# A list scheduler that weaves two layers together: two PSUM banks for the front, ranks of its evictions and of the carried columns' copies

## The chip, the core and the metric

The kernel runs on one core of a Trainium2 chip. The core has five engines with a queue of instructions each: PE (matmul, with its weight loads shown apart as PEld), DVE (vector), ACT (scalar functions), POOL (a second elementwise engine) and SP, which here issues nearly all DMAs. An engine takes its instructions in the order of its queue, and an instruction that waits holds up all that stand behind it. Matmuls write PSUM, which has eight banks of 128 x 512 float32; ACT and DVE read them there, POOL works on SBUF alone. The metric is the device time of one execution in microseconds.

## The reference, cut to what matters

Eight images of 56 x 56 x 192 go through two layers. Layer 0 is an attention whose queries and keys come from depthwise convolutions. Layer 1 is a selective scan in four directions. Everything is float32.

```python
def _L0_conv_ref(x, ...):                     # x is group-normalised before
    q  = _sep_conv(x, dw_q, ..., pw_q, 1)     # depthwise 3x3, batch norm, 1x1
    kv = _sep_conv(x, dw_kv, ..., pw_kv, 2)   # the same with stride 2
    k, v = jnp.split(kv, 2, axis=-1)
    scores = jnp.einsum('bihd,bjhd->bhij', q, k) * SCALE      # 3136 queries, 784 keys, 3 heads
    o = jnp.einsum('bhij,bjhd->bhid', jax.nn.softmax(scores, axis=-1), v)
    return jnp.einsum('bhwc,cd->bhwd', o, out_w) + out_b

def _ss2d(x, ...):                            # x is group-normalised before
    xa, z = jnp.split(jnp.einsum('bhwc,oc->bhwo', x, in_proj_w), 2, axis=-1)
    xc = jax.nn.silu(conv3x3_depthwise(xa) + conv_b)          # 384 channels
    xs = four directions of xc                                # rows, columns, and both reversed
    dts, Bs, Cs = jnp.split(jnp.einsum('bkdl,kcd->bkcl', xs, x_proj_weight), [R, R + N], axis=2)
    delta = jax.nn.softplus(dt_projs(dts) + bias)
    def step(h, inp):                                         # 3136 steps, 16 states per channel
        u_l, d_l, B_l, C_l = inp
        h = jnp.exp(d_l[..., None] * A) * h + d_l[..., None] * B_l[:, :, None, :] * u_l[..., None]
        return (h, jnp.sum(h * C_l[:, :, None, :], axis=-1))
    ...
    y = layernorm(sum of the four directions + xs * Ds) * jax.nn.silu(z)
    return jnp.einsum('bhwd,cd->bhwc', y, out_proj_w)

x = x + _L0_conv_ref(_gn(x), ...)
x = x + _L1_conv_ref(_gn(x), ...)
```

The four directions are put back in the order of the image before they are added.

## The kernel before

**Who sets the order.** The program has no fixed loop nest around its engines. While it is being built, a list scheduler (class `Sched`) runs some dozens of Python generators, called stages. A stage yields a request: an engine, an estimated duration, the cells that it reads and the cells that it writes. It may also ask for a buffer of a ring. The scheduler keeps a planned time for each engine, works out when each request could start, takes the one with the smallest start less rank, and lets its stage emit the instructions. A rank is thus a head start in microseconds: a request of rank 0.36 is taken before one of rank 0.16 as long as it starts no more than 0.2 later. What comes out is a fixed order for each engine; the chip then runs these orders with its own durations.

**The scan** (the stages in the list at line 1375) is a pipeline over `todo`: 8 images x 4 directions x 7 chunks of 448 positions x 16 states. For each of these 3584 steps:

- `inputs_made`: POOL multiplies the step sizes by a broadcast row of B into a state tile h (L1177, 128 x 1344). There are seven h tiles.
- `decays`: ACT makes three exponentials into da (L1191). These lie in PSUM banks.
- `scans`: DVE runs three scans (L1208) over da and h.
- `carries`: DVE copies the last column of h (L1230), from which the next chunk's scan of the same state starts, 16 steps on.
- `turned`, `scaled`, `back`: PE transposes h in four parts into a bank ht (L1255), ACT scales it by the C values (L1271), PE transposes it back and adds it up in three banks y of its own (L1289).
- `by_pool`: for four of the 16 states (three in the last image) POOL does the multiplication by C itself, from the second of a group on in place, into h (L1307), and adds up (L1311). It waits for the carry copy of that state, since the copy reads what L1307 may overwrite. `summed` adds the result into y on PE (L1326).
- `evicted`: DVE adds y to the image's sum (L1341, L1343).

`row_loads` fetches the B and C rows (tiles bb, five of them, and cb) over SP. An h tile is free when the copy and the turning, or the copy and POOL's product, are done.

**The front** is all that comes before the scan of an image: `front` (group norm, the first convolution L641 and L649, the projections L658 to L672, attention L784 and L793, the input projection L899, the second convolution L917) and `x_proj` (L994 to L1011). The front of image 0 and three chunks of its `x_proj` run alone with eight banks. After that, the front of image b + 1 runs beside the scan of image b, and `finish` (layer norm, gate, output projection, L1042 to L1094) beside both.

**Pacing.** `pace` says how much PE time the front should have used by the present place in the scan and how far it is behind. The scheduler skips a request of the front while the front is 12 or more ahead, and gives it a rank of 0.04 per microsecond behind, from 0 up to 0.45. The group of `finish` has a limit of its own, 0 in general.

**PSUM while both run.** Three banks are y. The other five are shared by three claims, each with a limit: da two, ht two, and one for the front and `finish` together. A request for a bank is answered when the claim is under its limit and one of the five is free.

**Fillers.** Where the planner sees PE idle, `warm` puts in small matmuls (L1421) that add zeros to y. One of them shows as two records in the profile.

The ranks of the scan's stages and the shared banks, as they stand before the change:

```python
            rda = share("da", 2)
            rht = share("ht", 2)
            banks[0] = share("bank1", 1)
            at["chunk"] = 0
            for g, rank in ((prepared, 0.3), (skips, 0.0), (row_loads, 0.25), (inputs_made, 0.0), (decays, 0.37),
                            (scans, 0.16), (carries, 0.36), (turned, 0.37), (scaled, 0.38), (by_pool, 0.39),
                            (back, 0.4), (summed, 0.0), (evicted, 0.71)):
```

Of the kernel before, what the change touches and what calls it, by code (L numbers as in the profile page):

```python
# [54 lines left out]
PE, ACT, DVE, POOL, SP = range(5)  # L55
# [3 lines left out]
URGENT = 0.45  # L59
AHEAD = 12.0  # L60
FIRM = 0.04


FILL = 64
# [103 lines left out]
class Sched:  # L168
# [54 lines left out]
    def run(self, until=None):  # L223
        while True:
            moved = True
            while moved:
                moved = False
                for s in list(self.stages):
                    while not s.done and not isinstance(s.req, tuple):
                        if isinstance(s.req, Ring):  # L230
                            if not s.req.ready():
                                break
                            self.resume(s, s.req.take())
                        else:
                            if not s.req():
                                break
                            self.resume(s)
                        moved = True
                    if s.done:
                        self.stages.remove(s)  # L240
                        moved = True
            if (until is not None and until()) or not self.stages:
                return
            best = None
            for s in self.stages:
                if not isinstance(s.req, tuple):
                    continue
                rank = s.rank
                if s.group in self.limit:
                    behind = self.limit[s.group]()  # L250
                    if behind <= -AHEAD:
                        continue
                    rank = max(rank, min(URGENT, FIRM * behind))
                e, _, reads, writes = s.req[:4]
                t = s.start
                for c in reads:
                    if c.w is None:
                        break
                    if c.w > t:
                        t = c.w  # L260
                else:
                    for c in writes:
                        if c.r > t:
                            t = c.r
                    t = max(t + HOP, self.at[e])
                    if best is None or t - rank < best[0]:
                        best = (t - rank, t, s)
            assert best is not None, "nothing can go on"
            _, t, s = best
            if s.req[0] == PE and self.filler is not None:  # L270
                self.keep_busy(t)
            self.give(s, t)
# [3 lines left out]
def kernel(  # L276
# [78 lines left out]
    for nm, src in (("q", bn_q), ("kv", bn_kv)):  # L355
        p = load(f"bn{nm}", [CP, 4, NB], src.rearrange("v (b p) -> p v b", p=CP))
        s = const.tile([CP, NB], F32, name=f"bns{nm}")
# [75 lines left out]
    banks = [None]  # L433
# [914 lines left out]
    with tc.manual_schedule():  # L1348
        order = [(lay, c) for lay in range(2) for c in range(NCH)]

        with tc.tile_pool(name="p8", bufs=8, space=PSUM) as p8:
            banks[0] = Ring(lambda: p8.tile([128, 512], F32, name="bank0"), 8)
            sc.spawn(front(0), 0.0, "front")
            sc.run()
            main = sc.spent.pop("front")
            sc.spawn(x_proj(0, order[:LEAD]), 0.0, "front")
            sc.run()
            each = sc.spent.pop("front") / LEAD

        with ExitStack() as es:  # L1360
            py = es.enter_context(tc.tile_pool(name="py", bufs=1, space=PSUM))
            pb = [es.enter_context(tc.tile_pool(name=f"pb{i}", bufs=1, space=PSUM)) for i in range(5)]
            ybanks = py.tile([128, NJ, 512], F32, name="y")
            nc.vector.memset(ybanks, 0.0)
            ry = Ring(lambda: ybanks, 1)
            shared = [Tile(1) for _ in pb]

            def share(name, most):
                return Share(shared, [lambda p=p: p.tile([128, 512], F32, name=name, tag="bank") for p in pb], most)

            rda = share("da", 2)
            rht = share("ht", 2)
            banks[0] = share("bank1", 1)
            at["chunk"] = 0
            for g, rank in ((prepared, 0.3), (skips, 0.0), (row_loads, 0.25), (inputs_made, 0.0), (decays, 0.37),
                            (scans, 0.16), (carries, 0.36), (turned, 0.37), (scaled, 0.38), (by_pool, 0.39),
                            (back, 0.4), (summed, 0.0), (evicted, 0.71)):
                sc.spawn(g(), rank, "scan")

            per = NDIR * NCH * NST  # L1380

            def ended(b):
                first = b * NDIR * NCH + (NDIR - 1) * NCH
                yield lambda: at["chunk"] >= first
                yield from finish(b, lambda c: lambda: at["chunk"] >= first + NCH - c, yread[b])

            def arounds():
                for b in range(nb):
                    yread[b] = {}
                    sc.spawn(ended(b), 0.0, "finish")  # L1390
                    if b > 0:
                        yield lambda: at["chunk"] >= b * NDIR * NCH
                    else:
                        yield from sc.join([sc.spawn(x_proj(0, order[LEAD:]), 0.0, "front")])
                    if b + 1 < nb:
                        yield from sc.join([sc.spawn(front(b + 1), 0.0, "front")])
                        yield from sc.join([sc.spawn(x_proj(b + 1, order), 0.0, "front")])

            def pace():

                b, slot = divmod(at["scan"], per)
                whole = main + len(order) * each
                lead = each * (len(order) - LEAD)
                before = b * whole + (lead if b else 0.0)
                here = whole + (0.0 if b else lead)
                late, share = (NDIR - 1) * NCH * NST, 0.87
                part = share * slot / late if slot < late else share + (1.0 - share) * (slot - late) / (per - 2 * NST - late)
                want = before + here * part
                return want - sc.spent.get("front", 0.0)

            def ending():
                done = sum(len(r) for r in yread.values())
                b, c = divmod(at["chunk"], NDIR * NCH)
                come = b * NCH + max(c - (NDIR - 1) * NCH, 0)
                return 1e9 if done < come - 1 or done < b * NCH else 0.0

            def warm():

                while True:
                    yield PE, T_FILL, [], []  # L1420
                    nc.tensor.matmul(ybanks[:, 0, T:T + FILL], zeros, zeros[:, :FILL], start=False, stop=False)  # L1421

            def may():
                y = ys.get(at["y"])
                return y is not None and y["left"][0] > 0 and y["on"]

            at["y"] = -1
            filler = Stage(warm(), 0.0, 0.0, None)
            sc.resume(filler)
            sc.filler = filler, may  # L1430
            sc.limit["front"] = pace
            sc.limit["finish"] = ending
            sc.spawn(arounds(), 0.0)
            sc.run()
# [58 lines left out]
```

## Time and profile before

| | |
|---|---|
| runs | 17156.64, 17158.03, 17169.37 us; median 17158.03 |
| the profiled execution | 17147.92 us, span 17146.2 us |
| granted PE clock, mean of that execution | 0.982 |
| h products on POOL, L1177 | x3584, 3054 ns each |
| scans on DVE, L1208 with a carry | x9216, 1136 ns each |
| decays on ACT, L1191 | x10752, 638 ns each |
| scaling on ACT, L1271 | x10864, 579 ns each |
| carry copies on DVE, L1230 | x3584, 158 ns each |
| fillers on PE, L1421 | x12432, 1600.3 us busy |
| HBM | read 1803.75 MB, written 550.97 MB |

How to read the profile: "busy" is the time in which an engine works on an instruction; the idle time before an instruction is put down to the one that released it ("<-"). Neighbours on ACT and DVE overlap a little, so the distance from start to start is shorter than the duration given. The same source line stands five lines further down in the changed kernel (two in the scheduler's first part). A wait put down to "issue" is one for which the profile shows no releaser.

### The profile page before, as it was taken

The numbers are of one execution on the slowest core, as the hardware profiler recorded it, in microseconds if no ns is written. First come the engines' busy times: TensorE is split into PE (matmuls) and PEld (weight loads), VectorE is DVE, ScalarE is ACT, GpSimd is POOL, SyncE is SP. The second block draws the span as 40 slices with busy tenths as digits, with TensorE's granted clock in tenths as the row PEclk, the third lists the DMA queues.
The fourth block names the chain that finished last, engine by engine and source line by source line (L and its number), as shares of the span: only waits on it lengthen the run. The fifth ranks groups of instructions, "written<-read, shape, count | busy, mean of one in ns | idle before, by whom it ended". The sixth has DMA issues, their size and how long they took to land. (4 is left out here: it accounts for less than half of the span.)

```text
span 17146.2 us, 283077 instructions
## 1 busy us (share of the span) xinstructions
PE 15622.8 (91%) x101664; PEld 10978.3 (64%) x101664; DVE 13834.8 (81%) x17783; ACT 14266.4 (83%) x25158; POOL 15542.8 (91%) x5200
## 2 busy tenths in 40 slices
PE   7699999999999999999899999999989999999998
PEld 3366666666666666666666666666666666667776
DVE  2378878888788878888788887888878888789998
ACT  3479888788888888888887888878888788888888
POOL 0389999899998999999898999989989899999998
PEclk9799999999999999999999999999999999999999
DMA  2653455436553365533745337453464534643332
GB/s 73 202 170 105 138 172 170 126 97 169 172 160 109 97 179 164 164 103 95 197 155 156 101 104 203 147 152 99 124 193 142 146 99 137 191 146 104 97 98 79
DMA packets 1508346, 2373.36 MB, mean 138 GB/s; under 512 B 197104, under 2 KB 1498912, under 8 KB 1503872
## 3 DMA queue, kind: packets, MB, share of 16 engines
q1 hardware_dynamic: 1506944, 2355.25, 47.3%
q8 instruction: 808, 13.24, 0.3%
q14 instruction: 594, 4.87, 0.1%
HBM read 1803.75 MB, written 550.97 MB: 137 GB/s over the span
## 5 line engine op out<-in xcount | busy, mean ns | idle before, releaser
L1208 DVE TENSOR_TENSOR_SCAN h<-da,newc,h 128x448 f32<-128x448 f32 x9216 | 10105.2, 1136 | 1535.2 <-ACT da L1191 1080.0
L1177 POOL TENSOR_TENSOR h<-du_s,bb 128x1344 f32<-128x1344 f32 x3584 | 10819.8, 3054 | 296.9 <-PE ht L1255 234.7
L1191 ACT ACTIVATE da<-dl_s,acoef 128x448 f32<-128x448 f32 x10752 | 6625.5, 638 | 766.6 <-DVE h L1208 454.0
L1271 ACT ACTIVATE g<-ht,ct_s 112x384 f32<-112x384 f32 x10864 | 5946.5, 579 | 1125.6 <-PE ht L1255 935.8
L1289 PE MATMUL y<-ident,g 112*128 112x112 f32 x32592 | 4889.8, 269 | 670.7 <-ACT g L1271 434.2
L1255 PE MATMUL ht<-ident,h 128*112 128x128 f32 x32592 | 5212.6, 277 | 232.0 <-DVE h L1208 169.5
L1289 PEld LDWEIGHTS y<-ident,g 112*128 112x128 f32 x32592 | 3524.6, 142 | 2752.1 <-ACT g L1271 1764.6
L1255 PEld LDWEIGHTS ht<-ident,h 128*112 128x112 f32 x32592 | 3699.3, 135 | 1185.9 <-issue 498.3
L1208 DVE TENSOR_TENSOR_SCAN h<-da,h 128x448 f32<-128x448 f32 x1536 | 1602.9, 1078 | 361.9 <-ACT da L1191 276.7
L1307 POOL TENSOR_TENSOR yp<-h,cb 128x1344 f32<-128x1344 f32 x448 | 1367.4, 3052 | 278.2 <-DVE h L1208 124.1
L1421 PEld LDWEIGHTS y<-zeros 128*128 128x128 f32 x12432 | 1553.3, 193 | 78.9 <-issue 78.9
L1421 PE MATMUL y<-zeros 128*128 128x64 f32 x12432 | 1600.3, 269 | 0.0
L1307 POOL TENSOR_TENSOR h<-h,cb 128x1344 f32<-128x1344 f32 x420 | 1282.1, 3053 | 271.3 <-issue 175.4
L1311 POOL TENSOR_TENSOR yp<-yp,h 128x1344 f32<-128x1344 f32 x420 | 1278.7, 3045 | 31.7
L784 PE MATMUL bank<-qT,kT 128*112 128x448 f32 x2352 | 1118.0, 568 | 115.6 <-ACT pT L734 48.7
L978 POOL TENSOR_TENSOR v<-v,xs 128x1344 f32<-128x1344 f32 x224 | 680.2, 3049 | 596.8 <-DMA dl<-v 584.0
L1326 PE MATMUL y<-yp,ident 128*128 128x448 f32 x2688 | 1205.0, 548 | 16.2 <-POOL yp L1311 15.9
L793 PE MATMUL bank<-pT,vt 112*128 112x448 f32 x2352 | 1038.7, 545 | 46.6 <-ACT pT L734 35.0
L734 ACT ACTIVATE pT<-bank,nsh 112x448 f32<-112x448 f32 x1176 | 744.5, 635 | 135.5 <-PE bank L784 118.9
L1011 PE MATMUL bank<-xd,dtw 128*128 128x448 f32 x1344 | 640.2, 561 | 25.1 <-DVE h L1208 12.7
L1230 DVE TENSOR_REDUCE newc<-h 128x3 f32<-128x3 f32 x3584 | 564.9, 158 | 107.8
L784 PEld LDWEIGHTS bank<-qT,kT 128*112 128x112 f32 x2352 | 346.6, 178 | 357.8 <-ACT pT L734 152.2
(147 smaller groups left out, 9664.2 us busy)
## 6 DMA issues: line engine op xcount, KB each, us to landing
bb<-rows SPq DMA_DIRECT2D x3584, 224.0 KB, 3.4
cb<-rows SPq DMA_DIRECT2D x868, 224.0 KB, 3.6
dl<-v SPq DMA_DIRECT2D x224, 672.0 KB, 4.9
du<-v SPq DMA_DIRECT2D x224, 672.0 KB, 6.2
du_s<-du SPq DMA_DIRECT2D x224, 672.0 KB, 4.7
dl_s<-dl SPq DMA_DIRECT2D x224, 672.0 KB, 4.7
stack<-xpd SPq DMA_DIRECT2D x504, 232.0 KB, 5.6
xt<-x1d SPq DMA_DIRECT2D x224, 336.0 KB, 5.0
```

Of the source, the lines that this page charges most:

```text
L784: nc.tensor.matmul(ps.ap[:TP, :T], kts[h][:, kb * TP:(kb + 1) * TP], qh.ap, start=True, stop=True)
L793: nc.tensor.matmul(po.ap[:, :T], vt[:, kb, g:g + 2, :].rearrange("p g d -> p (g d)"), pts[kb].ap, start=(kb == 0), stop=(kb == NKB - 1))
L1177: nc.gpsimd.tensor_tensor(h.ap, du.ap, bb.ap.unsqueeze(1).to_broadcast([128, NJ, T]), ALU.mult)
L1191: nc.scalar.activation(da.ap[:, :T], dl.ap[:, j], AF.Exp, scale=acoef[:, k * NJ + j, n:n + 1])
L1208: nc.vector.tensor_tensor_scan(h.ap[:, j, rev], da.ap[:, 0:T][:, rev], h.ap[:, j, rev], news[i - 1].ap[:, j, n:n + 1] if ci else 0.0, ALU. ...
L1255: nc.tensor.transpose(ht.ap[:TP, j * 128:(j + 1) * 128], h.ap[:, j, s * TP:(s + 1) * TP], ident)
L1271: nc.scalar.activation(g.ap, ht.ap[:TP, :DIN], AF.Copy, scale=ct.ap[:, s, n:n + 1])
L1289: nc.tensor.matmul(y["t"].ap[:, j, s * TP:(s + 1) * TP], g.ap[:, j * 128:(j + 1) * 128], ident[:TP, :TP], is_transpose=True, start=(n == 0 ...
L1307: nc.gpsimd.tensor_tensor(to.ap, h.ap, cbr.ap.unsqueeze(1).to_broadcast([128, NJ, T]), ALU.mult)
L1311: nc.gpsimd.tensor_tensor(yp.ap, yp.ap, h.ap, ALU.add)
L1326: nc.tensor.matmul(y["t"].ap[:, j, :T], ident, yp.ap[:, j], start=False, stop=(y["left"][j] == 0))
L1421: nc.tensor.matmul(ybanks[:, 0, T:T + FILL], zeros, zeros[:, :FILL], start=False, stop=False)
```

## The change

Three edits, all in what the scheduler is told. The front and `finish` may hold two of the five shared banks at once. The limit of a paced group, which applied to each of its requests, now applies only to requests for PE and to those whose estimated duration is over 1.0; the others (evictions of a bank, DMA issues, small vector work) are never held back for being ahead, and their rank is at least 0.2. And the copies of carried columns go from rank 0.36 to 0.25; the scans keep 0.16.

```diff
+EVICT = 0.2
+BRIEF = 1.0
...
                 if s.group in self.limit:
                     behind = self.limit[s.group]()
-                    if behind <= -AHEAD:
-                        continue
-                    rank = max(rank, min(URGENT, FIRM * behind))
+                    if s.req[0] == PE or s.req[1] > BRIEF:
+                        if behind <= -AHEAD:
+                            continue
+                        rank = max(rank, min(URGENT, FIRM * behind))
+                    else:
+                        rank = max(rank, EVICT, min(URGENT, FIRM * behind))
...
-            banks[0] = share("bank1", 1)
+            banks[0] = share("bank1", 2)
...
-                            (scans, 0.16), (carries, 0.36), (turned, 0.37), (scaled, 0.38), (by_pool, 0.39),
+                            (scans, 0.16), (carries, 0.25), (turned, 0.37), (scaled, 0.38), (by_pool, 0.39),
```

The constants here are `AHEAD` 12.0, `FIRM` 0.04 and `URGENT` 0.45.

## The prediction

> **What bounds the kernel now.** I read five views in this order: the page's busy table, the busy time by long stretch, the same by stretches of 100 us over one image, the waits of the engine found there, and the timeline of one such place.
>
> ```profile
> PE 15622.8 (91%) x101664; PEld 10978.3 (64%) x101664; DVE 13834.8 (81%) x17783; ACT 14266.4 (83%) x25158; POOL 15542.8 (91%) x5200
> ```
>
> ```profile
> 7200.00:9200.00 2000.00, 1844.94 (x11861) 1282.30 (x11860) 1651.05 (x2099) 1706.90 (x3006) 1887.37 (x630) 0.98 0.49 141
> 15200.00:16700.00 1500.00, 1361.96 (x10085) 1082.27 (x10084) 1341.38 (x1657) 1338.12 (x2449) 1494.27 (x497) 1.00 0.36 107
> ```
>
> The first line is the page's, the two others are long stretches. In these the pairs are PE, PE's weight load, DVE, ACT and POOL. POOL is the bound: with no front beside it (the last line) it is busy 1494 of 1500 us, with the front 1887 of 2000. PE's 91% flatters: the groups show 12432 filler records of 1600.3 us busy (two to an instruction), work that is put only into gaps, so useful PE work is 82%.
>
> POOL's instructions (5152 products of about 3.05 us) are untouched by the change. What can be won is its idle time: 17146.2 - 15542.8 = 1603 us, of which about 685 lie before the first h product (at 688 us, some set-up on POOL included) and 814 in 1200 to 15200. Where do the 814 lie?
>
> ```profile
> 7100.00:7200.00 100.00, 84.68 (x654) 71.59 (x653) 83.03 (x122) 70.87 (x131) 89.33 (x32) 0.96 0.64 183
> 7200.00:7300.00 100.00, 98.93 (x818) 61.03 (x818) 84.61 (x123) 69.22 (x129) 70.48 (x27) 0.99 0.59 158
> 7300.00:7400.00 100.00, 89.64 (x628) 64.37 (x626) 83.92 (x107) 78.11 (x149) 89.02 (x31) 0.95 0.37 105
> 7600.00:7700.00 100.00, 94.06 (x548) 62.70 (x547) 83.05 (x105) 89.77 (x166) 99.77 (x34) 1.00 0.36 108
> 8300.00:8400.00 100.00, 88.05 (x646) 53.62 (x638) 62.64 (x75) 77.58 (x124) 76.95 (x26) 0.90 0.75 194
> 8400.00:8500.00 100.00, 85.80 (x703) 61.17 (x702) 69.48 (x84) 92.57 (x158) 87.48 (x29) 1.00 0.70 202
> ```
>
> They lie in lumps. From 7100 to 7400 POOL loses 10.7 + 29.5 + 11.0 = 51 us, from 8300 to 8500 another 36; attention between them (7600) loses next to nothing. By line, 7200 to 7310 holds the front's first convolution (L641, L649; PE 98.9% busy), 8300 to 8450 its second (L917). Tagging all stretches of 100 us from 1000 to 15600 by these lines: the first convolution's lose 300.7 us over seven images (405 with their neighbours), the second's 220.3, attention's 156 (2.9 per 100 us), the rest 169.
>
> ```profile
> POOL h L1177 <- PE ht L1255: 16.4, 6, 7.5
> POOL h L1307 <- issue: 10.1, 3, 7.0
> POOL yp L1307 <- DVE h L1208: 9.3, 2, 6.8
> POOL h L1307 <- DVE newc L1230: 7.4, 2, 5.9
> ```
>
> ```profile
> 7225.53 0.64 ACT L1191 ACTIVATE da<-dl_s,acoef 128x448 f32<-128x448 f32 x1 [1.87 <-DVE hkv L595]
> 7227.82 0.72 ACT L614 ACTIVATE hq<-bank,bntq,bnsq 96x448 f32<-96x448 f32 x1 [0.60 <-PE bank L649]
> ```
>
> The first four are POOL's waits in 7100 to 7400 (total, times, longest): no state buffer is free because PE turns states late, or a scan or carry copy is late. The last two are ACT there: a decay waits 1.87 us for the bank that an eviction of the front gives back, then an eviction waits for its matmul.
>
> **What the Trainium skill says.** "Perfetto Trace Analysis", Optimizing Tensor Performance, Matmuls, says that independent groups should rotate through PSUM banks so that evacuation lies beside the next matmuls; the bracketed waits above agree that one bank does not give that. Its Optimization Strategy says to look at regimes apart, and the table by stretch is why. "Trainium Architecture — The Big Picture", Inside one NeuronCore, says that each engine has its own stream and they meet at semaphores; so an order fixed beforehand stalls wherever the chip is later than the plan. In the trace a scan costs 1.08 us from start to start (3.24 for three) against the planner's 1.065, a decay 0.60 against 0.56, a scaling 0.52 against 0.47.
>
> **The change part by part.** The program after has the same instructions on ACT, DVE, POOL and SP; only PE's fillers fall, 6216 to 5785. All else is order, so I compared the two programs' orders, counting place in h products (one each 4.4 us in a front image: 651 POOL instructions x 3.05 / 448). The first image's lone front, 700 us, is untouched.
>
> *Second bank and prompt evictions.* Before, the chunk h 48 to 64 of an image holds 53.9 us of front PE work (each instruction at its mean in the trace) and no filler: the front starts late (inputs turned at h 22 to 29, convolution at 42 to 65), is behind its pace, and takes the rank 0.45 that beats everything of the scan but adding up a chunk. After, inputs are turned at h 5 to 17, the convolution spans 29 to 59, and the densest chunk of that stage has 32.8 us, then 25.9 and 25.1. Attention has 25 us per chunk in both, at 2.9 us of POOL lost per 100 us. Between 25 us costing 2.9 and 53.9 costing 29.5 a line gives about 10 at 32.8; the stage would cost 10 + 3 + 3 = 16 instead of 51, a gain of 35 per image. The 7100 stretch also has the image's boundary, and the two bounds are 0 (the loss only moves) and 51; I take 27. 7 x 27 = 190 us. The second convolution keeps its density (31.6 to 32.9): 0, bounds +-10 per image, +-70 in all. x_proj ends at h 417 instead of spilling to the next image: no engine waited much there, 0.
>
> *What the banks cost.* Five banks now serve 2 + 2 + 2 claims. In building, the front takes its bank with one already held in 2437 of 3399 cases, and ht has to start from none held in 1181 of 10864 (4 before). That can hurt: see the first rival. I take 0 for what the new order has absorbed, with up to +350 kept.
>
> *Evictions past the pace.* What is not on PE and costs under 1.0 also goes on when the front is ahead. On SP these are DMAs (0.32 us each to issue); the lead of the bb loads over the h products is the same in both orders (lead of one: 353 and 350 times), so bb's 23.3 us of waits should stay: 0, up to +40. On ACT and DVE rank 0.2 still stands under decays (0.37) and scalings (0.38) but over scans (0.16): a scan late by one 0.6 us copy is hidden by DVE's 17% idle.
>
> *Carries.* Before, every copy L1230 follows its own third scan; after, 1686 of 3131 follow the next step's first scan. It removes a stall that the planner sees (0.13 us after the scan) and the trace hardly does: 107.8 us idle over 3584 copies, on an engine that is not the bound: 0 to -50. Behind the copy wait POOL's in-place products L1307. If 54% of the 49 + 81 waits of 1200 to 15200 that are named newc or issue grow by one scan, 0.54 x 130 x 1.08 = 76 us; the new order may put the product later, then 0. I take +20.
>
> *Last image.* No front, but 1267 fillers instead of 1098: 169 x 0.257 = 43 us of PE. PE has 138 us idle in the 1500 there and POOL binds: 0, at worst +43. *The end:* finish may hold two banks, -2 us at most, taken as 0.
>
> Sum: -190 + 20 - 20 (fewer waits of attention's evictions, 0 to -60 from its 156) = -190. The profiled execution took 17147.9, span 17146.2; that gives 16958. The median of the runs is 10 us above it, so I say 16965. The fillers speak for the same size: a front image has 100 fewer (719 to 619), 100 x 0.257 = 26 us less room on PE per image, though they are a plan's gaps and not the chip's.
>
> **The rivals.** *The turning loop loses its second bank (slower).* While the front holds two banks and the decays two, ht has one, and PE's turn, ACT's scaling and the hand-overs run one after another: 0.49 + 0.58 + about 0.2 = 1.27 us per tile. A front chunk allows 23 x 3.05 / 48 = 1.46. If one decay of 0.60 stands in the loop every other time, it is 1.57, 0.11 too much; the share of decays taken in that state is 3655 of 10752, 34%, so of 7 x 28 x 48 = 9408 tiles 3200 pay 0.11: 350 us, less the 190 won, and 17320. It decides from 1.46 us per tile. For it: POOL already waits 217 us for PE's turns in 1200 to 15200. Against: that order was made with the banks counted.
>
> *The loss only moves (no change).* The front's PE work per image is the same, and the chip's lateness against the plan may make as many holes spread as in lumps: 17150. Against: attention shows that 25 us per chunk goes nearly free.
>
> *Both convolutions heal (larger gain).* With two banks ACT no longer meets the matmul at the bank, and POOL loses attention's 3% everywhere: 350 + 70 = 420 us, 16740. Against: the second convolution also waits for its stack loads.
>
> *The banks do nothing* is excluded by the 2437 second takes.
>
> **How the numbers follow.** Forecast 0.53, from 16850 to 17080 or a little above; larger gain 0.15; no change 0.07; slower 0.25. The runs of a kernel differ by some 0.1%, and what can be told from no change is 0.2%, 34 us. Faster 0.68, same 0.07, slower 0.25. With 16760 to 17240 I leave out the larger gain's end (0.06) and the worse half of the slower case (0.13).
>
> **What would show it.** Right: POOL's busy stays at 15540; in the stretches of the first convolution it loses under 15 us per 100 instead of 30; the second still loses about 12 to 23; PE's fillers fall to 11570 records. Wrong: waits of L1177 for ht at L1260 well above 235 us, or ACT's scalings waiting longer than 936 us for PE, mean the loop; waits of L1312 for the copies above 170 us mean the carries; holes of POOL inside attention mean that the loss moved.

## The result and the profile after

The changed kernel took 17014.25 us, the median of four runs (17000.83 to 17024.88), against 17159.81 before: a ratio of 0.9914 with a 95% interval of 0.9897 to 0.9931. That is 0.86% less, 146 us. The profiled execution has a span of 16999.1 us, 147.1 shorter. Three lines of its page and of its stretches answer to the first ones of before; the pairs are again PE, PE's weight load, DVE, ACT and POOL.

```profile
PE 15535.8 (91%) x100802; PEld 10839.1 (64%) x100802; DVE 13629.1 (80%) x17783; ACT 14233.1 (84%) x25158; POOL 15540.0 (91%) x5200
```

```profile
7200.00:9200.00 2000.00, 1845.02 (x11786) 1280.26 (x11786) 1646.89 (x2128) 1717.61 (x3026) 1902.93 (x637) 0.98 0.48 144
15200.00:16700.00 1500.00, 1361.56 (x10511) 1124.82 (x10509) 1325.33 (x1670) 1331.40 (x2494) 1495.11 (x498) 1.00 0.33 101
```

POOL is as busy as before, 15540 us. Nearly the whole difference is its idle time: 17146.2 - 15542.8 = 1603 before, 16999.1 - 15540.0 = 1459 after, 144 us less. So the question is which holes in POOL went. One image of after, in stretches of 100 us:

```profile
7000.00:7100.00 100.00, 90.63 (x707) 69.10 (x708) 82.44 (x122) 80.79 (x147) 91.83 (x35) 0.98 0.74 220
7100.00:7200.00 100.00, 96.78 (x750) 63.18 (x744) 79.86 (x115) 75.69 (x143) 76.08 (x26) 0.98 0.46 135
7200.00:7300.00 100.00, 84.93 (x621) 59.03 (x620) 92.79 (x113) 74.92 (x142) 97.74 (x33) 0.95 0.41 122
8100.00:8200.00 100.00, 94.86 (x613) 54.37 (x611) 84.12 (x109) 74.84 (x133) 84.06 (x29) 0.99 0.89 237
```

The first three hold the first convolution: POOL loses 8 + 24 + 2 = 34 us where it lost 51. The lump is smaller, but it is there; the last line begins the second convolution. Tagged as in the prediction, over all stretches from 1000 to 15600:

| POOL idle, us | before | after |
|---|---|---|
| first convolution (with the neighbouring stretches) | 300.7 (405) | 267.1 (348) |
| second convolution | 220.3 | 223.8 |
| attention | 156.2 | 103.1 |
| the rest | 169.0 | 122.2 |
| sum | 846 | 716 |

The tags move a little: the second convolution has 23 stretches after and 18 before, the rest 52 and 58, so part of the rest's fall is a change of tags.

What is left of the lump looks different. POOL's waits in 7000 to 7300 of after (total, times, longest), and then lines of the timeline of its longest hole (start, duration, idle before):

```profile
POOL h L1312 <- issue: 24.8, 4, 14.3
POOL h L1312 <- DVE newc L1235: 5.0, 3, 3.8
POOL h L1182 <- PE ht L1260: 4.0, 3, 2.4
```

```profile
7103.53 0.22 DVE L613 COPY vt<-bank 112x64 f32<-112x64 f32 x1 [1.36 <-PE bank L669]
7108.04 3.22 DVE L1213 TENSOR_TENSOR_SCAN h<-da,newc,h 128x448 f32<-128x448 f32 x3
7108.15 0.64 ACT L1196 ACTIVATE da<-dl_s,acoef 128x448 f32<-128x448 f32 x1 [2.47 <-DVE hkv L600]
7111.68 1.15 DVE L1213 TENSOR_TENSOR_SCAN h<-da,newc,h 128x448 f32<-128x448 f32 x1 [0.43 <-ACT da L1196]
7112.75 0.37 DVE L600 TENSOR_SCALAR hkv<-bank,bnskv,bntkv 96x112 f32<-96x112 f32 x1
7113.04 0.14 DVE L1235 TENSOR_REDUCE newc<-h 128x3 f32<-128x3 f32 x1
7113.32 3.06 POOL L1312 TENSOR_TENSOR h<-h,cb 128x1344 f32<-128x1344 f32 x1 [14.26 <-issue]
```

The wait named "issue" ends as the carry copy of 7113.04 ends (0.14 us later), so it is a wait for a copy. That holds beyond this hole: of the 66 waits of in-place products named issue in 1200 to 15000, 64 end within 0.3 us after a copy. Before, POOL stood for turns and for copies alike; after, most of what it waits here (30 of 37 us) is the in-place product L1312 behind a late copy.

The copy is late because of what DVE does in these 14.3 us. Besides seven scans it works off eight pieces of the front, some 3.3 us, and waits 1.36 us for the matmul of one of them. The copy itself stands behind the next step's first scan and one more piece: it starts 1.8 us after its own third scan has ended at 7111.26. A decay did wait 2.47 us until DVE had emptied a bank of the front, but DVE runs the three scans from 7108.04 without a break, and its only wait for a decay here is 0.43 us.

### The profile page after: what moved, and what is told of

Its sections match the earlier page's. It is cut to its first block, busy times and chain, and to the rows that moved or that the text cites. A ratio compares the mean times of both kernels' runs of the same rounds, so it can differ in the third digit from the quotient of the medians.

```text
span 16999.1 us, 281592 instructions
## 1 busy us (share of the span) xinstructions
PE 15535.8 (91%) x100802; PEld 10839.1 (64%) x100802; DVE 13629.1 (80%) x17783; ACT 14233.1 (84%) x25158; POOL 15540.0 (91%) x5200
## 5 line engine op out<-in xcount | busy, mean ns | idle before, releaser
L1260 PE MATMUL ht<-ident,h 128*112 128x128 f32 x32592 | 5281.3, 279 | 329.5 <-DVE h L1213 124.3
L1312 POOL TENSOR_TENSOR h<-h,cb 128x1344 f32<-128x1344 f32 x420 | 1284.0, 3057 | 451.0 <-issue 293.8
L1426 PEld LDWEIGHTS y<-zeros 128*128 128x128 f32 x11570 | 1462.0, 196 | 75.2 <-issue 75.2
L1426 PE MATMUL y<-zeros 128*128 128x64 f32 x11570 | 1500.4, 272 | 0.0
L1312 POOL TENSOR_TENSOR yp<-h,cb 128x1344 f32<-128x1344 f32 x448 | 1368.7, 3055 | 102.0 <-DVE h L1213 44.6
L1316 POOL TENSOR_TENSOR yp<-yp,h 128x1344 f32<-128x1344 f32 x420 | 1278.4, 3044 | 32.8
L789 PE MATMUL bank<-qT,kT 128*112 128x448 f32 x2352 | 1077.8, 550 | 57.7 <-DVE h L1213 42.6
L1331 PEld LDWEIGHTS y<-yp,ident 128*128 128x128 f32 x2688 | 438.1, 191 | 177.8 <-issue 160.3
L1235 DVE TENSOR_REDUCE newc<-h 128x3 f32<-128x3 f32 x3584 | 509.3, 142 | 34.3
```

Source lines behind the costliest of these rows:

```text
L789: nc.tensor.matmul(ps.ap[:TP, :T], kts[h][:, kb * TP:(kb + 1) * TP], qh.ap, start=True, stop=True)
L1260: nc.tensor.transpose(ht.ap[:TP, j * 128:(j + 1) * 128], h.ap[:, j, s * TP:(s + 1) * TP], ident)
L1312: nc.gpsimd.tensor_tensor(to.ap, h.ap, cbr.ap.unsqueeze(1).to_broadcast([128, NJ, T]), ALU.mult)
L1316: nc.gpsimd.tensor_tensor(yp.ap, yp.ap, h.ap, ALU.add)
L1331: nc.tensor.matmul(y["t"].ap[:, j, :T], ident, yp.ap[:, j], start=False, stop=(y["left"][j] == 0))
```

## The experiments

Each starts from the changed kernel and puts edits back, or changes one number. All ratios are against the kernel before.

**The three edits alone.** Each of the first three runs keeps one edit of the change and puts the other two back; the fourth puts back the copies' rank alone, by the line shown. Theory A is the prediction's.

> Only the second bank for the front and finish; evictions paced as before, copies at rank 0.36. Theory A (the lumps: the front starts earlier and its first convolution is spread, bank and evictions together do it): about half of the gain, -60 to -120 us against before, and POOL's idle in the stretches of the first convolution falls. Rival B (the carries' lower rank is what gains, since the planner no longer sees a stall of DVE after each third scan): within 40 us of before. Rival C (the turning loop's lost bank costs): slower than before by 50 us or more, and POOL's waits for ht rise above 235 us.

> Only the evictions' own rank and their release from the pace; one bank, copies at rank 0.36. Theory A: -60 to -120 us against before, as the front's start moves from h 22 to h 12 of an image and its densest chunk stays at 53.9 us of PE work. Rival B: within 40 us of before. If the densest chunk sets the loss of the first convolution's stretches, that loss stays near 300 us here and falls in the run with the banks alone.

> Only the copies' rank 0.36 to 0.25. Theory A: slower than before by 50 to 100 us, since POOL's in-place products wait for copies that come one scan later: their waits named newc and issue rise from 313 us in 1200 to 15200 to about 400. Rival B: faster than before by 80 us or more.

```diff
-                            (scans, 0.16), (carries, 0.25), (turned, 0.37), (scaled, 0.38), (by_pool, 0.39),
+                            (scans, 0.16), (carries, 0.36), (turned, 0.37), (scaled, 0.38), (by_pool, 0.39),
```

> The changed kernel with the copies' rank put back to 0.36: both other edits stay. Theory A: faster than the changed kernel by 60 to 100 us (near 16930), with the waits of the in-place products for copies back at about 310 us from 412. Rival B: slower than the changed kernel by 80 us or more (17100 or above).

| kernel | median us | ratio and interval |
|---|---|---|
| second bank alone | 17122.4 | 0.9980 (0.9972 to 0.9987) |
| eviction rank alone | 17119.0 | 0.9976 (0.9968 to 0.9984) |
| copies' rank alone | 17139.4 | 0.9988 (0.9979 to 0.9996) |
| bank and eviction rank, copies back at 0.36 | 16944.5 | 0.9875 (0.9861 to 0.9888) |
| all three (the change) | 17014.3 | 0.9914 (0.9897 to 0.9931) |

Each alone gives 20 to 40 us, less than A expected of the first two and the other sign than it expected of the third. The first two lie in B's range of 40 us, but B also asked for 80 us or more from the third and for 17100 or more with the copies back, and neither came. Nor did C: POOL's waits for turns were 224 us with the banks alone. In the run of the third the waits of POOL's products by C (L1312, those into yp among them) for copies did rise, from 311 to 413 us in 1200 to 15000, but those for a free h tile fell from 217 to 157 and those of the products into yp for scans from 117 to 71. Together, bank and eviction rank give 214 us, nearly three times their sum. And the copies' lower rank, a small gain alone, costs about 70 us on top of the two. The kernel with the copies back beats both kernels of this case. POOL's waits in 1200 to 15000 show the exchange, first before, then in the changed kernel, then with the copies back:

```profile
POOL h L1177 <- PE ht L1255: 217.4, 82, 9.2
POOL h L1307 <- issue: 164.2, 58, 10.0
POOL h L1307 <- DVE newc L1230: 71.7, 32, 8.6
```

```profile
POOL h L1312 <- issue: 266.4, 66, 14.7
POOL h L1312 <- DVE newc L1235: 115.0, 44, 7.8
POOL h L1182 <- PE ht L1260: 91.1, 56, 5.5
```

```profile
POOL h L1312 <- issue: 203.0, 69, 10.0
POOL h L1312 <- DVE newc L1235: 44.6, 40, 2.8
POOL h L1182 <- PE ht L1260: 167.8, 68, 5.5
```

With late copies POOL waits 134 us more at the in-place product and 77 less for a free h tile; 57 us of the 70 are in these three lines.

**Density is worth little.** How long is PE busy with the front while POOL makes 14 h products in a row, at the densest place of the first convolution? In the traces, for the last five of the seven images with a front beside them: 60 us before, 46 to 47 in the change, 45 to 46 with two banks alone, 46 to 50 with the eviction rank alone. Each half spreads the burst about as much as the change does. With the banks alone the first convolution still loses 272 us (372 with the neighbours), which is 29 of the 34 us that the change saves there; with the eviction rank alone it loses 285. So flattening the burst brings some 30 us, and the gain of the pair lies elsewhere:

| POOL idle, us | before | two banks alone | eviction rank alone | both, copies at 0.36 |
|---|---|---|---|---|
| first convolution | 300.7 | 272.2 | 285.3 | 246.5 |
| second convolution | 220.3 | 285.3 | 243.0 | 228.0 |
| attention | 156.2 | 130.1 | 152.4 | 83.7 |
| the rest | 169.0 | 125.6 | 156.0 | 95.9 |
| sum | 846 | 813 | 837 | 654 |

With the banks alone three rows gain and the second convolution loses 65 us. The trace shows where: POOL waits for rows of B, most of it in one hole of 11 to 13 us in the second convolution of five images. The first line is the sum in 1200 to 15000, the others are one of these holes:

```profile
POOL h L1182 <- DMA bb<-rows: 73.6, 11, 12.7
```

```profile
10476.51 2.46 SPq L489 DMA_DIRECT2D xcw<-xw  x2
10488.41 2.06 SPq L489 DMA_DIRECT2D stack<-xpd  x3
10500.05 3.05 POOL L1182 TENSOR_TENSOR h<-du_s,bb 128x1344 f32<-128x1344 f32 x1 [11.80 <-DMA bb<-rows]
```

SP issues nothing from 10478.97 to 10488.41: it waits to issue a stack load of the front until PE's L922 has used the old stack, and the loads of B stand behind it. With the rank beside the banks POOL's waits for B are 2.0 us. So this stall accounts for about 70 of the 159 us of idle time that the rank takes from POOL here; why the order with the rank avoids it was not traced.

**Which queue the rank works on.** Two banks, copies at 0.36, and the rank for one engine's brief requests at a time:

```diff
-                    if s.req[0] == PE or s.req[1] > BRIEF:
+                    if s.req[0] != DVE or s.req[1] > BRIEF:
```

> Two banks, copies at 0.36, and the rank of at least 0.2 only for the front's brief requests on DVE. The two banks alone gave 17122, with the rank on all three queues 16945. Theory D (the rank works through DVE's evictions: 0.2 puts them before the scans' 0.16, so a bank comes back to the turning sooner): most of the 178 us, 17000 or less. Rival S (it works through SP, whose requests fall under the same rank): within 40 us of the two banks alone, 17080 to 17160.

> The same with the rank only for the front's brief requests on ACT. Theory D: 17080 to 17160, since 0.2 still stands under decays (0.37) and scalings (0.38) there. Rival A (ACT's evictions free the banks of the convolutions and of the scores): 17030 or less.

> The same with the rank only for the DMA issues of the front. Theory D: 17080 to 17160, with POOL's waits for the bb rows still near 74 us as with the two banks alone. Rival S: 17030 or less, and those waits fall to 15 us or less as in the run with the copies back.

DVE gave 0.9958 (0.9945 to 0.9972), ACT 0.9972 (0.9961 to 0.9982), SP 0.9973 (0.9965 to 0.9981), against 0.9980 without the rank. DVE has the largest share, 0.22%, but not most of the gain as D expected, and the intervals of ACT and SP overlap that of no rank; the three add up to 0.37% of the 1.05% that the rank brings on all three queues. POOL's wait for the B rows (bb) stayed at 75 us on SP alone, so rival S falls too, and ACT did not reach what rival A asked. With DVE alone these waits were 28 us, with ACT alone 14.

The other half of that edit does nothing. A program in which brief requests are freed from the pace but get no rank of their own is, on all five engines, instruction for instruction the one with the banks alone: the front is never 12 ahead.

**The copies, state by state.**

```diff
             h = states[i, n][0]
+            sc.now.rank = 0.36 if n in by[i] else 0.25
             yield DVE, 0.08, h.c[1:1 + NJ], [news[i].c[n]]
```

> The changed kernel, but the copies of the states that POOL multiplies by C keep rank 0.36; the others have 0.25. Theory W (the copies' lower rank costs because POOL's in-place product waits for a copy that comes one scan later): at or under the 16945 of the run with all copies back, and POOL's waits named newc and issue before the in-place products fall from 412 us to about 300. Rival P (the copies' rank matters through the whole plan, by whatever order comes out): stays within 40 us of the changed kernel's 17014 or above it.

16948.6 us, 0.9882 (0.9868 to 0.9895): the 70 us are back, though in an image with a front 12 of 16 copies keep the lower rank. So the rank of the other four decides the time. That it does so through the products' waits for copies is shown only in part: they fell from 412 to 351 us, where W put about 300.

**Who owns the banks.** The decays get two of the five for themselves (the added numbers are the first bank of a claim and the end of its range):

```diff
-            rda = share("da", 2)
-            rht = share("ht", 2)
-            banks[0] = share("bank1", 2)
+            rda = share("da", 2, 0, 2)
+            rht = share("ht", 2, 2)
+            banks[0] = share("bank1", 2, 2)
```

> Base is the changed kernel with the copies back at 0.36 (16945). Here the decays keep two of the five banks for themselves, and the front and the turning share the other three, two each at most. Theory F (what the second bank brought is that decays no longer wait for the front's evictions: ACT's idle before decays put down to them fell from 187 to 64 us): the wait goes to near 0, and the time stays within 40 us of 16945 or falls. Rival G (five banks to all is what counts, the lending itself): slower than 16945 by 60 us or more, with ACT's scalings waiting longer for PE's turns than 694 us in 1200 to 15000.

17180.7 us, 1.0008 (1.0000 to 1.0016). The decays' waits for the front's evictions went to 0 as F says, and all of the gain was gone. In 1200 to 15000 decays now wait 739 us for scans (479 with five shared banks), and scalings 824 us for turns (694). So rival G came: without the decays' lending the gain is gone. That the lending by itself is the gain is not shown, since the turning is now the only lender: counted in the program's order, it starts with no bank of its own 1676 times, with five shared banks 1102 times.

**POOL's product planned later.** `SLACK` is 3.0; the lines below are cut at the dots.

```diff
             if n in by[i]:
+                late[i, n] = Cell()
+                late[i, n].w = news[i].c[n].w + SLACK
...
-            yield POOL, t_pool(NJ * T), h.c[1:1 + NJ] + [news[i].c[n]] + cbr.c, ...
+            yield POOL, t_pool(NJ * T), h.c[1:1 + NJ] + [news[i].c[n], late.pop((i, n))] + cbr.c, ...
```

> Same base. The planner takes the carry copy as ready 3 us later than it does now, for POOL's product by C alone, so that POOL's order holds more h products before it; nothing is computed otherwise. Theory W (POOL loses what it waits at the product, 298 us of its 654 idle in 1000 to 15600): these waits fall below 150 us and the time by 60 us or more. Rival H (the h tiles are held longer, and POOL waits for a free one instead): the waits before h products for PE's turns rise from 168 us by as much, and the time stays within 40 us or rises.

17009.8 us, 0.9910 (0.9894 to 0.9925), slower than its base. The waits moved, as H says:

```profile
POOL h L1183 <- PE ht L1264: 332.1, 119, 9.5
POOL h L1318 <- issue: 83.8, 21, 9.2
```

The products' waits for copies fell from 298 to about 150 us, and those for a free h tile rose from 168 to 332.

**A higher rank, and an eighth h tile.** `EVICT` 0.45, and `HBUFS` 8:

> Same base, the rank of the front's brief requests at 0.45 instead of 0.2, over decays, scalings and turnings. If the sooner return of the bank is what the rank brings (theory D), then 16945 or less, with less waiting of PE's front matmuls for evictions than 149 us. If evictions in front of decays cost the scan (rival), 17000 or more, with DVE waiting longer for decays than 1169 us in 1200 to 15000.

> The changed kernel with the copies back at 0.36 and with eight h tiles instead of seven. Theory B (POOL's holes are the lateness of the whole loop of DVE, ACT and PE against a fixed order, over what the h tiles can cover; the waits moved from the product to the h product when the product was planned later): one more tile covers one more product of 3.05 us, so POOL's idle in 1000 to 15600 falls from 654 us by 100 or more, and the time to 16850 or less. Rival (the waits are for scans and copies that come late in DVE's own order, which a further tile doesn't move): within 40 us of 16945.

The rank of 0.45 gave 17002.5 us, 0.9904 (0.9890 to 0.9917). The rival's two signs came: the time, and scans that wait 1433 us for decays instead of 1169. But their waits for POOL's h products fell at the same time, from 432 to 110 us, so the scans do not wait longer in all; the decay is now what comes last. PE's matmuls of front and `finish` wait less for ACT and DVE (100 us for 149). The eighth tile gave 16985.0 us, 0.9894 (0.9877 to 0.9910), whose interval meets that of seven tiles; the hundred microseconds that theory B asked of it did not come, and it lies at the edge of the 40 us that the rival left. So the holes are not simply lateness that one more tile would cover.

**What was not tried: the clock.** PE's granted clock differs between these programs: 0.979 to 0.980 in the runs of the change, 0.983 to 0.986 with the copies back, 0.985 to 0.986 state by state, 0.976 to 0.980 with the decays' own banks. The unchanged kernel's time goes with its clock too: of its 37 runs beside the first experiments, 11 at 0.982 have a median of 17173.5 us and 11 at 0.984 one of 17145.6. By this slope, an estimate, the 0.005 between the change and the copies back would go with some 70 us, all that the copies' rank costs. Whether the order lowers the clock and the clock the speed, or the late copies lower both, no run separates.

## Why the prediction was right, and where not

*Direction and bound were right, the size by luck.* -146 us was measured, -190 said. POOL binds; its busy time did not move, and the gain is its idle time. Fillers came out at 11570 records, as the order had it.

*The first convolution, -190, is the term that failed.* Its stretches gave 57 us with their neighbours, 8 per image and not 27. The step that failed is the line from PE work per chunk to POOL's loss. Its input was too good: chunks at fixed places showed 53.9 us against 32.8, while the densest 14 products in a row fall only from 60 to 47. And its slope was too steep: the run with the banks alone has the flat burst and saves 29 us in these stretches, 36 us in all. The densest stretch of the image shown still loses 24 us, where I had asked for under 15. Most of the time went in attention, -53 us, and the rest, -47; I had put 20 there. The sum came near by luck: what was too large in one place was too small in others.

*The turning loop's second bank, the slower rival, did not bind.* POOL's waits for turns fell from 217 to 91 us, and ACT's scalings wait less for turns in 1200 to 15000, as the lines of before and after show:

```profile
ACT g L1271 <- PE ht L1255: 841.1, 1240, 5.6
```

```profile
ACT g L1276 <- PE ht L1260: 766.7, 1347, 4.7
```

That the front holds two banks at a third of the decays was read rightly from the order; that this would bind was not.

*The evictions' rank was taken at nothing apart from 20 us.* It is half of a pair. Beside two banks it is worth 1.05%, alone 0.24%. In 1200 to 15000 it cuts the waits of PE's matmuls of front and `finish` for ACT and DVE from 201 to 149 us; of these, 114 and 73 are put down to scans, scalings and copies, so the waits for evictions themselves fall only from 87 to 76. Waits of scans for decays go from 1310 to 1169. I tried its parts by engine, and no part alone has it.

*The carries, +20 with +76 as the bound,* came out at about +70 beside the two other edits, and at -20 alone. Late copies were the mechanism named, and the waits moved that way; the clock above is a rival. The waits of L1312 named newc passed the mark of 170 us only together with those named issue, which were waits for copies in all but two cases.

*The second convolution at 0, SP at 0, the last image at 0* held: 220.3 to 223.8; bb's waits 15 us in 1200 to 15000, 10.7 before; POOL busy 1495 of 1500 in the last image. The first two came out only with the rank beside the banks: with the banks alone the second convolution loses 65 us more, and the waits for bb are 63 us longer.

*The chip behind the plan* was misread. A scan was put at 1.08 us from start to start by dividing 3.24 by three, which counts the last one's overlap in full. Between starts of neighbours without a gap the median of before is 1.06 for a scan, 0.56 for a decay and 0.48 for a scaling, against 1.065, 0.56 and 0.47 in the plan. Where POOL's holes come from is thus not answered by slower instructions.

*Open.* Why bank and rank give three times their sum (214 us against 76) is settled in part: the stall of the B rows, about 70 us of POOL's idle time, comes with the banks alone and goes with the rank. For the remainder two things are shown: without the decays' lending the gain is gone, and no single queue's rank has it. A chain that fits both, not shown, is that a second bank held for long starves turns and decays, and the rank shortens the holding. In the order, turning asks for a bank with the front holding two 2462 times with the banks alone, 2123 with the rank, and starts with none of its own 1477 and 1102 times. This was counted, not tried by itself.

## What to carry to other kernels

Give a stage more buffers and a higher rank for its short requests, which free them, as one edit, and try edits in pairs as well as alone: here either alone showed a sixth to a fifth of what both gave. A planner's cure for a stall that the trace doesn't have (the 0.13 us after a third scan) can cost real time where another engine's fixed order stands behind the moved instruction; here moving only the copies that POOL does not wait for cost nothing that could be told. A further buffer can also move a stall to another queue: look at the waits of every engine, the DMA queue among them, before calling it useless. And a wait at a fixed place in a queue may be only where a whole loop's lateness shows: planning that place later moved 150 us of waits to the next one and won nothing.

## What was not expected of the hardware

No measurement stands out as new of the chip itself. An eighth state tile, which allows one more product of 3.05 us ahead, did not shorten the time, and giving two banks to one user cost some 230 us (1.0008 against 0.9875) beside sharing all five.
